# Two-layer vision network in one program: the routing of layer 0's mixture of experts is rewritten and its slot writes leave their critical sections

## The chip, the cores and the metric

The kernel runs on one core of a Trainium2 chip, as one program with one launch. The metric is the device time of one execution in microseconds (us); the median of three runs stands for a kernel. Beside the times there is one execution recorded by the hardware profiler, with every instruction of the five engines: PE (TensorE, matrix products), DVE (VectorE), ACT (ScalarE), POOL (GpSimd) and SP (SyncE, which here only starts DMA transfers). "ACTq", "POOLq" and the like are the instruction queues of an engine, from which DMA transfers are started too.

## The reference, cut to what matters

The network has two layers, each a token mixer and a mixture of experts, on 4 images of 256 channels and 32 x 32 positions (4096 tokens in all). Layer 0 mixes by attention and then sends each token to the best two of eight experts. Each layer normalises the tokens ahead of this, without gain or bias; then:

```python
logits = tokens.astype(jnp.float32) @ router_w.astype(jnp.float32).T
probs = jax.nn.softmax(logits, axis=-1)
rw, re = jax.lax.top_k(probs, TOP_K)
if TOP_K > 1:
    rw = rw / jnp.maximum(rw.sum(-1, keepdims=True), 1e-12)
...
for e in range(E):
    h = jax.nn.gelu(tokens @ w1[e] + b1[e], approximate=False)
    y = h @ w2[e] + b2[e]
    out = out + combine[:, e:e + 1] * y
```

The two weights are the probabilities of the best two, divided by their sum. Written with the logits l1 >= l2 of the two they are 1 / (1 + exp(l2 - l1)) and exp(l2 - l1) / (1 + exp(l2 - l1)): the softmax over all eight cancels. And since a token's mean is the same for all channels, the product of the centred token with the router is the product of the token itself with router weights whose mean over the channels has been taken out.

## The kernel before, in words

Notation: P = 128 partitions, C = 256 channels in CT = 2 halves, L = 1024 positions of an image in NT = 8 tiles of 128 tokens, B = 4 images, E = 8 experts. The activations of all images stay in SBUF, as x[b], 128 x (2 x 1024), channels on partitions.

The program has stages that follow each other: normalisation and attention of layer 0; the routing of layer 0; its experts (tiles of 256 slots); the scans of layer 1, which carry the routing of layer 1 beside them; the experts of layer 1; the output. Attention and scans are emitted in an order written out by hand. The routing and the experts of layer 0 are emitted plainly, and the framework's scheduler decides the order of the instructions within each engine; it also inserts the semaphores, and it gives the DMA transfers of POOL eight semaphores in turn. A buffer pool with a given number of buffers makes a new tile wait until the oldest one is free. After attention a conditional block (line 1021) holds a second, slower attention, which is not taken here; the routing comes behind it.

**Routing of one image** (loop at line 1543, per image): `norm` (line 1253) multiplies x[b] by a matrix of 1/C on PE, which gives each token's mean on all partitions (L1262); DVE subtracts it (L1265) into d; PE transposes d, so that tokens lie on partitions (L1274), and multiplies d by the router weights rw0 (L1276); DVE copies the logits out of PSUM (L1278), ACT copies the rows into `tok` (L1279), and squares them with a running sum for the variance (L1282). The inverse root comes from ACT's Sqrt (L1290), a reciprocal on DVE (L1292) and one Newton step (L1293 to L1296). Logits (L1301) and rows (L1304, ACT, 8 instructions) are multiplied by it. `route` (line 1131) makes the softmax (L1158 to L1163, its Exp on ACT at L1160), and takes the best expert twice (`best`, L1150 to L1154). The weights of both go into columns C + 1 and C + 2 of the row (L1176 to L1181). Then it counts, by two products on PE (L1193, L1194) and running sums on DVE (L1197 to L1213), which place of its expert each token gets; the slot numbers go as integers into `here` (L1217 to L1219). The logits of all images lie in one tile, lg1; `here` and the scratch tile `numbers` have one buffer too.

**Slot writes.** Each row is 259 numbers long: 256 channels, the best expert's number and two weights. POOL writes the rows of an image into the slots of their experts in DRAM (slots_x0): 8 tiles x 2 choices = 16 transfers of 128 rows each, with addresses from `here` (L1557). They stand in a critical section (L1554) on POOL, at whose end POOL waits until all 16 have landed:

```python
with tc.tile_critical(name=f"scatter{b}", no_gpsimd_drain=True):
    for n in range(NT):
        for k in range(2):
            nc.gpsimd.indirect_dma_start(
                out=slots_x0, out_offset=bass.IndirectOffsetOnAxis(ap=here[:, k, n : n + 1], axis=0),
                in_=tokens[b][:, n], in_offset=None).then_inc(scattered, 16)
    nc.gpsimd.wait_ge(scattered, 16 * 2 * NT * (b + 1))
```

**Experts of layer 0** (line 1656 on): `load` (L1583 to L1588) starts, on SP and in this order, the rows of a tile, then its two weight matrices; PE transposes the rows (L1594), multiplies by w1 (L1616), ACT takes the GELU (L1618), PE multiplies by w2 (L1624), DVE and ACT add bias and weight (L1627 to L1632), POOL starts the store (L1634). The first tile needs the rows of all images. Other small loads that the change touches are started on ACT, by the helper `load` at line 83 (L85): the weights of the attention at the start of the program, and at the start of the routing those of the scans (wd, wbc, bd, dskip, a_log) and the bias b1_0.

## Time and profile before

| | us |
|---|---|
| median of three runs | 4119.95 |
| the three runs | 4119.56, 4119.95, 4127.55 |
| the profiled execution, its time | 4116.54 |
| its span, from first to last instruction | 4114.8 |
| attention's last addition to x, ended | 1899.1 |
| first matmul of the routing (L1262) | 1904.73 |
| first and last slot write (L1557), started | 1937.46, 2039.19 |
| first load of an expert tile's rows (L1583), started | 2042.63 |
| first GELU of layer 0's experts (L1618) | 2049.41 |

Over the whole span PE is busy for 86%, DVE for 74%, ACT for 69% and POOL for 43%. A page of the profile gives these shares for the whole, and in 40 slices of 103 us each; the routing lies in slices 19 and 20. In a timeline each line is: start, duration, engine, line of the program, operation, output and inputs, count; and in brackets the idle time of the engine before it and what ended that. In the list of waits a line says who waited for whom, the total, the number of times and the longest. The release that is named is inferred: where a wait had several conditions, it is the one that came last in the record.

### The profile page before, as it was taken

How to read it: one execution, taken by the hardware profiler on the slowest of the kernel's cores; microseconds unless marked ns; L12 is line 12 of the kernel's file. 1: busy time of each engine (PE TensorE's matmuls, PEld its weight loads, DVE VectorE, ACT ScalarE, POOL GpSimd, SP SyncE). 2: the span in 40 equal slices, each digit the busy share in tenths (PEclk: the TensorE clock that was granted, in tenths of full speed). 3: DMA queues.
4: the chain of work that ended last, by engine and by line, in shares of the span. 5: the costliest groups of instructions: out<-in, count | busy, mean ns of one | idle time of the engine just before them, and what ended most of it. 6: DMA issues, size and time to landing. Idle time of an engine off the chain costs nothing. (4 is left out here: it accounts for less than half of the span.)

```text
span 4114.8 us, 50233 instructions
## 1 busy us (share of the span) xinstructions
PE 3526.9 (86%) x17502; PEld 1947.5 (47%) x17502; DVE 3032.4 (74%) x5416; ACT 2828.4 (69%) x3805; POOL 1785.3 (43%) x1435
## 2 busy tenths in 40 slices
PE   8378888888888888965388999999999999999996
PEld 5134444444344434433275444444444434688885
DVE  2689899989898989893466899899899899411112
ACT  2889999999999999973234676767667677422222
POOL 0145444554455445552433656445445446121111
PEclk9568787888778877887699999999999999999997
DMA  9300093000000000000384434333323334555565
GB/s 288 97 1 1 1 255 90 1 1 19 1 1 1 11 1 1 10 2 31 107 241 140 133 110 133 103 108 125 107 99 124 117 102 138 187 183 190 189 194 181
DMA packets 241817, 393.33 MB, mean 96 GB/s; under 512 B 31889, under 2 KB 182162, under 8 KB 241426
## 3 DMA queue, kind: packets, MB, share of 16 engines
q1 hardware_dynamic: 217872, 340.19, 27.3%
q0 software_dynamic: 19904, 48.42, 3.6%
q8 instruction: 141, 2.31, 0.2%
q10 hardware_dynamic: 3778, 1.41, 0.1%
q14 instruction: 122, 1.00, 0.1%
HBM read 280.34 MB, written 109.61 MB: 95 GB/s over the span
## 5 line engine op out<-in xcount | busy, mean ns | idle before, releaser
L491 POOL TENSOR_SCALAR dr<-s_n,last 128x1024 bf16<-128x1024 f32 x256 | 733.0, 2883 | 853.7 <-DVE state L519 392.3
L407 ACT ACTIVATE junk_a<-s_n,state 128x1024 int8<-128x1024 f32 x448 | 514.6, 1149 | 24.8 <-DVE state L525 7.5
L1768 POOL TENSOR_TENSOR da_c<-prod,come 128x1024 f32<-128x1024 f32 x128 | 247.5, 1934 | 436.1 <-DVE h L1774 376.4
L411 DVE TENSOR_SCALAR_CACHE_REDUCE junk_v<-s_n,state 128x1024 int8<-128x1024 f32 x320 | 408.6, 1277 | 8.8
L1944 ACT ACTIVATE hid<-hp,b 128x256 f32<-128x256 f32 x288 | 133.8, 474 | 356.2 <-PE hp L1942 353.3
L458 DVE SCALAR_TENSOR_TENSOR w<-s_n,win 128x1024 f32<-128x1024 f32 x256 | 349.2, 1364 | 5.3
L461 DVE MAX8 win<-w 128x8 f32<-128x1024 f32 x256 | 314.5, 1228 | 8.9
L559 ACT ACTIVATE ex<-sT 128x1024 f32<-128x1024 f32 x256 | 247.0, 1015 | 87.3 <-PE sT L551 87.2
L1735 POOL TENSOR_TENSOR uu<-dx,bb 128x1024 f32<-128x1024 f32 x127 | 302.3, 2380 | 1.9 <-DMA bb<-bc_d 1.7
L407 ACT ACTIVATE junk_a<-s_n,guess 128x1024 int8<-128x1024 f32 x256 | 294.2, 1149 | 7.4
L1774 DVE TENSOR_TENSOR_SCAN h<-da_c,uu 128x1024 f32<-128x1024 f32 x127 | 288.7, 2273 | 0.0
L1748 DVE TENSOR_TENSOR_SCAN h<-da,uu 128x1024 f32<-128x1024 f32 x127 | 288.4, 2271 | 0.0
L1757 DVE TENSOR_TENSOR_SCAN h<-da,uu 128x1024 f32<-128x1024 f32 x127 | 287.4, 2263 | 0.0
L569 PE MATMUL o_ps<-ex,vT 128*32 128x256 f32 x2048 | 241.5, 451 | 46.2 <-ACT ex L559 38.8
L1719 ACT ACTIVATE da_c<-delta,a_log 128x1024 f32<-128x1024 f32 x128 | 268.4, 2097 | 6.6 <-issue 6.5
L1778 PE MATMUL hp<-h,ident 128*128 128x512 f32 x512 | 250.4, 612 | 22.8 <-DVE h L1774 22.6
L1942 PE MATMUL hp<-xe,w 128*128 128x256 f32 x1152 | 258.8, 381 | 7.3 <-DVE xe L1930 7.1
L441 ACT COPY s_n<-sp 128x1024 f32<-128x1024 f32 x256 | 245.4, 1003 | 22.4 <-PE sp L433 11.5
L1953 DVE TENSOR_TENSOR ys<-yp,b2e 128x512 f32<-128x512 f32 x36 | 24.9, 692 | 319.6 <-PE yp L1950 319.6
L1950 PE MATMUL yp<-w2e,hid 128*128 128x256 f32 x1152 | 255.9, 379 | 0.0
L1743 PE MATMUL hp<-da_c,ident 128*128 128x512 f32 x512 | 248.8, 609 | 6.3 <-POOL da_c L1768 3.6
L1736 ACT COPY uu<-uu 128x1024 f32<-128x1024 f32 x127 | 252.5, 1988 | 1.6 <-POOL uu L1735 1.6
(570 smaller groups left out, 7471.6 us busy)
## 6 DMA issues: line engine op xcount, KB each, us to landing
cb<-bc_d SPq DMA_DIRECT2D x128, 512.0 KB
bb<-bc_d SPq DMA_DIRECT2D x127, 512.0 KB
w<-in_w SPq DMA_DIRECT2D x36, 1024.0 KB
w2e<-in_w SPq DMA_DIRECT2D x36, 1024.0 KB
slots_x<-zeros SPq DMA_DIRECT2D x1, 33411.0 KB
slots_x<-zeros SPq DMA_DIRECT2D x1, 33282.0 KB
w<-in_w SPq DMA_DIRECT2D x72, 256.0 KB
xs<-slots_x SPq DMA_DIRECT2D x36, 259.0 KB
```

The lines of the kernel that those rows point to most:

```text
L407: nc.scalar.activation(junk, self.row(r), AF.Sign, bias=thr, scale=-1.0, accum_out=u)
L411: nc.vector.tensor_scalar(junk, self.row(r), thr, None, ALU.is_lt, ALU.add, accum_out=u)
L458: nc.vector.scalar_tensor_tensor(w, self.row(r), self.win[:, r, 0:1], self.row(r), ALU.is_gt if r < LAST_DVE else ALU.is_ge, ALU.subtract, ...
L461: nc.vector.max(out=self.win[:, r, 1:], in_=w)
L491: ins = nc.gpsimd.tensor_scalar(dr, self.row(r), self.last[:, r : r + 1], None, ALU.is_lt)
L1719: nc.scalar.activation(grid(self.da_c), cols_flipped(self.prep.delta[:, self.c]), AF.Exp, scale=self.decay)
L1735: nc.gpsimd.tensor_tensor(self.uu[:, 0], self.prep.dx[:, self.c], self.bb, ALU.mult)
L1748: nc.vector.tensor_tensor_scan(rows.rearrange("p r w -> p (r w)"), self.da, self.uu[:, 0], 0.0, ALU.mult, ALU.add)
L1757: nc.vector.tensor_tensor_scan(hs[:, ::-1], self.da[:, ::-1], self.uu[:, 0][:, ::-1], 0.0, ALU.mult, ALU.add)
L1774: nc.vector.tensor_tensor_scan(hs, self.da_c, self.uu[:, 1], 0.0, ALU.mult, ALU.add)
L1942: nc.tensor.matmul(hp[:, f % 2], self.w1[:, c, ts(f, P)], self.xe[:, c], start=(c == 0), stop=(c == CT - 1))
L1950: nc.tensor.matmul(yp[:, a], self.hid[:, f, ts(a, P)], self.w2[:, f, :], start=(f == 0), stop=(f == NF - 1))
```

## The change

- The router weights are loaded at the very start of the program, their mean over the channels is taken out (two products on PE, one subtraction on DVE), and a ninth column of 1/C is added: one product of a token with it gives the logits and the mean.
- A new function `normed0` takes the place of `norm` in layer 0. It works on x[b] directly: products with the nine columns for all tiles of an image in one PSUM tile (`raw`, two buffers), transposes into three buffers `t`; DVE makes minus the mean from the ninth column, ACT copies the rows and squares them with the mean as a bias. The inverse root is made on DVE alone, by a first guess from the bits and three Newton steps. ACT then scales and shifts the rows (8 instructions).
- `route` in layer 0 takes the best two from the logits. One Exp, of l2 - l1, 8 numbers per token row, is left, and the weights are made from it after the counting products.
- Logits, `here`, scratch and small tiles have two or four buffers, where they had one.
- The critical sections go. The 64 slot writes are declared as free of dependences on each other ("rows of their own"); the loads of the experts wait for them by the framework's semaphores.
- Six small loads (wd, wbc, bd, dskip, a_log, b1_0) move from ACT's queue to SP's, ahead of the load of b2_0.

In the order that the build gives, PE makes the products of image 1 between those of image 0, and a slot write waits for the one eight before it, for ACT's scaling of its rows and for `here`. `norm` keeps layer 1's part, with its argument for the layer taken away; the two calls that follow from this are left out below.

```diff
     nc.gpsimd.iota(zeros[:, C : C + 1], [[0, 1]], base=2 * B * L, channel_multiplier=2,
                    allow_small_or_imprecise_dtypes=True)
 
+
+    rw0 = cons.tile([P, CT, E + 1], F32, tag="rw0", name="rw0")
+    nc.vector.memset(rw0[:, :, E:], 1.0 / C)
+    with tc.tile_pool(name="w_ps", bufs=1, space=PSUM) as pool_p, tc.tile_pool(name="w_sb", bufs=1) as pool_s:
+        raw0 = load(pool_s, "raw0", [P, CT, E], t["rw0"].rearrange("(c p) o -> p c o", p=P))
+        mean = pool_p.tile([P, E], F32, tag="mean", name="mean")
+        for c in range(CT):
+            nc.tensor.matmul(mean, mean_w, raw0[:, c], start=(c == 0), stop=(c == CT - 1))
+        nc.vector.tensor_tensor(rw0[:, :, :E], raw0, mean.unsqueeze(1).to_broadcast([P, CT, E]), ALU.subtract)
 
     kf = cons.tile([P, 1], F32, tag="kf", name="kf")
...
     rt = ctx.enter_context(tc.tile_pool(name="rt", bufs=1))
     rw1 = load(cons, "rw1", [P, CT, E], t["wr1"].rearrange("(c p) o -> p c o", p=P))
     brs = load(cons, "brs", [P, E], t["br1"][0].partition_broadcast(P))
-    rw0 = load(cons, "rw0", [P, CT, E], t["rw0"].rearrange("(c p) o -> p c o", p=P))
     def kept(name, shape, dt=F32):
         return rt.tile([P, *shape], dt, tag=name, name=name)
...
     every, early, late = Tiles("every", NTILE), Tiles("early", EARLY), Tiles("late", NTILE - EARLY)
     extra = rt.tile([1, 1], I32, tag="extra", name="extra")
 
-    def route(b, layer, tok, slot, space, psum, tag, keep_hots=None, keep_rank=None):
+    def route(b, layer, tok, slot, space, psum, tag, lg1=lg1, keep_hots=None, keep_rank=None):
 
 
         used = 0
...
             nc.vector.tensor_reduce(red, eq, AX.X, ALU.max)
             nc.vector.tensor_tensor(hot, eq, red.unsqueeze(2).to_broadcast(wide), ALU.is_equal)
 
-        if layer == 0:
-
-            nc.vector.tensor_reduce(m1, lg1, AX.X, ALU.max)
-            nc.vector.tensor_tensor(lg1, lg1, m1.unsqueeze(2).to_broadcast(wide), ALU.subtract)
-            nc.scalar.activation(lg1, lg1, AF.Exp)
-            nc.vector.tensor_reduce(m1, lg1, AX.X, ALU.add)
-            nc.vector.reciprocal(m1, m1)
-            nc.vector.tensor_tensor(lg1, lg1, m1.unsqueeze(2).to_broadcast(wide), ALU.mult)
-        else:
+        if layer == 1:
             nc.vector.tensor_tensor(lg1, lg1, brs.unsqueeze(1).to_broadcast(wide), ALU.add)
         best(m1, hot1)
         yield
...
         nc.vector.scalar_tensor_tensor(lg1, hot1, -1e30, lg1, ALU.mult, ALU.add)
         best(m2, hot2)
         hots = (hot1, hot2)
-        if layer == 0:
-            nc.vector.tensor_tensor(red, m1, m2, ALU.add)
-            nc.vector.tensor_scalar(red, red, 1e-12, None, ALU.max)
-            nc.vector.reciprocal(red, red)
-            nc.vector.tensor_tensor(m1, m1, red, ALU.mult)
-            nc.vector.tensor_tensor(tok[:, :, C + 2], m2, red, ALU.mult)
-            nc.vector.tensor_tensor(tok[:, :, C + 1], m1, tok[:, :, C + 2], ALU.subtract)
-        else:
-            nc.vector.tensor_tensor(m2, m2, m1, ALU.subtract)
-            nc.scalar.activation(m2, m2, AF.Exp)
-
+        nc.vector.tensor_tensor(m2, m2, m1, ALU.subtract)
+        nc.scalar.activation(m2, m2, AF.Exp)
         both, tote, keep, cum = room([NT, E]), room([E, NT]), room([E, NT]), room([E, NT])
         nc.vector.tensor_tensor(both, hot1, hot2, ALU.add)
         yield
...
         nc.vector.tensor_scalar(tote, sums[:, 1].rearrange("p n e -> p e n"), float(C), None, ALU.mult)
         nc.vector.tensor_copy(place, sums[:, 0].rearrange("p n e -> p e n"))
         yield
-        if layer == 1:
+        if layer == 0:
+            nc.vector.tensor_scalar(red, m2, 1.0, None, ALU.add)
+            nc.vector.reciprocal(m1, red)
+            nc.vector.tensor_tensor(tok[:, :, C + 2], m2, m1, ALU.mult)
+            nc.vector.tensor_tensor(tok[:, :, C + 1], m1, tok[:, :, C + 2], ALU.subtract)
+        else:
             nc.vector.tensor_scalar(m1, m2, 1.0, None, ALU.add)
             nc.vector.reciprocal(wts[:, 0, ts(b, NT)], m1)
             nc.vector.tensor_tensor(wts[:, 1, ts(b, NT)], m2, wts[:, 0, ts(b, NT)], ALU.mult)
...
             ends = late.fill(room, tiles, done)
             nc.vector.tensor_scalar(extra, ends[0:1, E - 1 : E], USUAL - EARLY + 0.5, None, ALU.is_gt)
 
-    def norm(b, layer, tok, pool, psum, tag, raw_tag, d):
-
-
-
-        rw = (rw0, rw1)[layer]
+    def normed0(b, tok, lg, pool, psum):
+
+        raw = psum.tile([P, HALF], F32, tag="raw", name="raw")[:, : NT * (E + 1)].rearrange(
+            "p (n e) -> p n e", e=E + 1)
+        ve, rr, r0, rs, nm = (pool.tile([P, NT], F32, tag=f"n0_{i}", name=f"n0_{i}")
+                              for i in ("ve", "rr", "r0", "rs", "nm"))
+        for r in range(NT // 2):
+            tp = psum.tile([P, 2, C], F32, tag="t", name="tp", bufs=3)
+            for i in range(2):
+                n = 2 * r + i
+                for c in range(CT):
+                    nc.tensor.matmul(raw[:, n], x[b][:, c, ts(n, P)], rw0[:, c, :], start=(c == 0), stop=(c == CT - 1))
+                for c in range(CT):
+                    nc.tensor.transpose(tp[:, i, ts(c, P)], x[b][:, c, ts(n, P)], ident)
+            nc.vector.tensor_scalar(nm[:, ts(r, 2)], raw[:, ts(r, 2), E], -C ** -0.5, None, ALU.mult)
+            nc.scalar.copy(tok[:, ts(r, 2), :C], tp)
+            for i in range(2):
+                n = 2 * r + i
+                nc.scalar.activation(tp[:, i], tp[:, i], AF.Square, bias=nm[:, n : n + 1], scale=C ** -0.5,
+                                     accum_out=ve[:, n : n + 1])
+        nc.vector.tensor_scalar(ve, ve, 1e-5, None, ALU.add)
+        nc.vector.tensor_scalar(r0.bitcast(I32), ve.bitcast(I32), -0.5, RSQRT_BITS, ALU.mult, ALU.add)
+        for src, dst in ((r0, rs), (rs, r0), (r0, rs)):
+            nc.vector.tensor_tensor(rr, src, src, ALU.mult)
+            nc.vector.scalar_tensor_tensor(rr, rr, -0.5, ve, ALU.mult, ALU.mult)
+            nc.vector.scalar_tensor_tensor(dst, rr, 1.5, src, ALU.add, ALU.mult)
+        nc.vector.tensor_tensor(lg, raw[:, :, :E], rs.unsqueeze(2).to_broadcast([P, NT, E]), ALU.mult)
+        nc.vector.scalar_tensor_tensor(nm, nm, C ** 0.5, rs, ALU.mult, ALU.mult)
+        for n in range(NT):
+            nc.scalar.activation(tok[:, n, :C], tok[:, n, :C], AF.Identity, bias=nm[:, n : n + 1],
+                                 scale=rs[:, n : n + 1])
+
+    def norm(b, tok, pool, psum, tag, raw_tag, d):
+
+
+
+        rw = rw1
         for h in range(NHALF):
             cols = ts(h, HALF)
             mean = psum.tile([P, HALF], F32, tag=tag, name="nm_mean")
...
         nc.vector.tensor_scalar(ve, var, 1e-5, None, ALU.add)
         yield from rsqrt(s1)
-        if layer == 0:
-            nc.vector.tensor_tensor(lg1, lg1, s1.unsqueeze(2).to_broadcast([P, NT, E]), ALU.mult)
-            yield
-            for n in range(NT):
-                nc.scalar.mul(tok[:, n, :C], tok[:, n, :C], s1[:, n : n + 1])
-            yield
-            return
-
         nc.vector.tensor_tensor(ve, s1, s1, ALU.mult)
         nc.vector.tensor_tensor(ve, ve, var, ALU.mult)
         nc.vector.tensor_scalar(ve, ve, 1e-5, None, ALU.add)
...
     sd = of_scans.enter_context(tc.tile_pool(name="s_d", bufs=2))
     sw = of_scans.enter_context(tc.tile_pool(name="s_c", bufs=1))
     bc_dram = ctx.enter_context(tc.tile_pool(name="s_dram", bufs=2, space=bass.MemoryType.DRAM))
-    wd = load_rows(sw, "wd", C)
-    wbc = load_rows(sw, "wbc", 2 * NS)
-    bd = load(sw, "bd", [P, CT])
-    dsk = load(sw, "dskip", [P, CT])
-
-    am = load(sw, "a_log", [P, CT, NS])
+    wd = load_rows(sw, "wd", C, nc.sync)
+    wbc = load_rows(sw, "wbc", 2 * NS, nc.sync)
+    bd = load(sw, "bd", [P, CT], eng=nc.sync)
+    dsk = load(sw, "dskip", [P, CT], eng=nc.sync)
+
+    am = load(sw, "a_log", [P, CT, NS], eng=nc.sync)
     nc.scalar.activation(am, am, AF.Exp)
     nc.vector.tensor_scalar(am, am, -1.0, None, ALU.mult)
     twice = sw.tile([P, P], F32, tag="twice", name="twice")
...
     with ExitStack() as st:
         wp = st.enter_context(tc.tile_pool(name="m0_w", bufs=1))
-        b1 = load(wp, "b1_0", [P, E, CT])
+        b1 = load(wp, "b1_0", [P, E, CT], eng=nc.sync)
         b2 = wp.tile([P, E, C], F32, tag="b2_0", name="b2_0")
         nc.sync.dma_start(b2, t["b2_0"].rearrange("e d -> (e d)").partition_broadcast(P).rearrange(
             "p (e d) -> p e d", e=E))
...
         with ExitStack() as sr:
             pr = sr.enter_context(tc.tile_pool(name="r0_w", bufs=1))
             pd = sr.enter_context(tc.tile_pool(name="r0_b", bufs=2))
-            ps_n = sr.enter_context(tc.tile_pool(name="r0_ps", bufs=3, space=PSUM))
-            tokens = [pr.tile([P, NT, W0], F32, tag=f"tok{b}", name=f"tok{b}") for b in range(B)]
-            scattered = nc.alloc_semaphore("scattered")
+            ps_n = sr.enter_context(tc.tile_pool(name="r0_ps", bufs=2, space=PSUM))
             for b in range(B):
                 hots0.append([wp.tile([P, NT, E], F32, tag=f"hot{b}{k}", name="hot") for k in range(2)])
                 rank0.append(wp.tile([P, E, NT], F32, tag=f"rank{b}", name="rank"))
-                d = pd.tile([P, CT, L], F32, tag="d", name="d")
-                here = pr.tile([P, 2, NT], I32, tag="here", name="here")
-                for _ in norm(b, 0, tokens[b], pd, ps_n, "t", "t", d):
+                rows = pr.tile([P, NT, W0], F32, tag=f"tok{b}", name="rows")
+                lg = pd.tile([P, NT, E], F32, tag="lg", name="lg")
+                here = pd.tile([P, 2, NT], I32, tag="here", name="here", bufs=B)
+                normed0(b, rows, lg, pd, ps_n)
+                numbers = pd.tile([P, 1408], F32, tag="numbers", name="numbers")
+                for _ in route(b, 0, rows, here, numbers, ps_n, "r", lg, hots0[b], rank0[b]):
                     pass
-                numbers = pr.tile([P, 1408], F32, tag="numbers", name="numbers")
-                for _ in route(b, 0, tokens[b], here, numbers, ps_n, "t", hots0[b], rank0[b]):
-                    pass
-
-                with tc.tile_critical(name=f"scatter{b}", no_gpsimd_drain=True):
-                    for n in range(NT):
-                        for k in range(2):
-                            nc.gpsimd.indirect_dma_start(
-                                out=slots_x0, out_offset=bass.IndirectOffsetOnAxis(ap=here[:, k, n : n + 1], axis=0),
-                                in_=tokens[b][:, n], in_offset=None).then_inc(scattered, 16)
-                    nc.gpsimd.wait_ge(scattered, 16 * 2 * NT * (b + 1))
-                    if b == B - 1:
-                        nc.clear_and_free_semaphores([scattered])
+                for n in range(NT):
+                    for k in range(2):
+                        ins = nc.gpsimd.indirect_dma_start(
+                            out=slots_x0, out_offset=bass.IndirectOffsetOnAxis(ap=here[:, k, n : n + 1], axis=0),
+                            in_=rows[:, n], in_offset=None).ins
+                        tc.declare_no_dep(ins, group="scatter0", reason="rows of their own")
+                        tc.add_to_no_dep_group("scatter0", ins)
 
         pb = st.enter_context(tc.tile_pool(name="m0_b", bufs=2))
         ps_n = st.enter_context(tc.tile_pool(name="m0_ps_n", bufs=3, space=PSUM))
```

More of the change, by code (lines that the diff above doesn't have):

```diff
@@ L86, in load, with load_rows @@
         return w
-    def load_rows(pool, name, cols):
-        return load(pool, name, [P, CT, cols], t[name].rearrange("(c p) o -> p c o", p=P))
+    def load_rows(pool, name, cols, eng=None):
+        return load(pool, name, [P, CT, cols], t[name].rearrange("(c p) o -> p c o", p=P), eng)
     def layer_norm_steps(dst, src, eps, room, psum, tag):
@@ L1811, in routed @@
             nonlocal sending
-            yield from norm(b, 1, tok, p1, ps_m, "hp", "hp", p1.tile([P, CT, L], F32, tag="xm", name="nm_d"))
+            yield from norm(b, tok, p1, ps_m, "hp", "hp", p1.tile([P, CT, L], F32, tag="xm", name="nm_d"))
             yield from route(b, 1, tok, slot, p1.tile([P, NUMBERS], F32, tag="numbers", name="numbers"), ps_m, "hp")
@@ L1976, in metaformer @@
             b = B - 1
-            routing = chain(norm(b, 1, tok, pa, psa, "t", "raw", pa.tile([P, CT, L], F32, tag="nm_d", name="nm_d")),
+            routing = chain(norm(b, tok, pa, psa, "t", "raw", pa.tile([P, CT, L], F32, tag="nm_d", name="nm_d")),
                             route(b, 1, tok, slot, pa.tile([P, NUMBERS], F32, tag="numbers", name="numbers"), psa, "t"), scatter(b))
```

## The prediction

> **What bounds the kernel now.** I read the page for the shares by slice, the waits and the timelines of each engine around the routing of layer 0, and the windows by stage. The page's chain of work that ended last is almost all from the last stage, so the routing has to be judged in its own window. Attention ends at 1899, the branch after it costs until 1904.7, the first tile of layer 0's experts is loaded at 2042.6. In most of those 138 us all engines are lightly used:
>
> ```profile
> core 0: us, PE busy (x) PEld busy (x) DVE busy (x) ACT busy (x) POOL busy (x), PEclk, DMA share, GB/s
> 1937.00:2042.00 105.00, 34.66 (x178) 26.48 (x176) 36.95 (x193) 36.27 (x96) 61.79 (x64) 0.61 0.23 81
> ```
>
> POOL is the busiest, with the 64 slot writes (L1557), and even it idles. The waits of 1900 to 2045 (waiter, what released it, total us, times, longest):
>
> ```profile
> ACT L1618 <- POOLq L1554: 33.0, 1, 33.0
> POOL slots_x L1557 <- PE nm_mean L1262: 31.1, 1, 31.1
> POOL slots_x L1557 <- issue: 18.3, 60, 0.3
> POOL slots_x L1557 <- DVE d L1265: 14.5, 2, 8.2
> POOL slots_x L1557 <- SPq L1638: 8.1, 1, 8.1
> ```
>
> The first line is the experts' start: it waits for POOL's last critical section. POOL's own timeline shows the rest: within an image one write per 1.265 us (0.96 busy, 0.30 between), between images a hole.
>
> ```profile
> 1937.46 1.26 POOL L1557 DMA_INDIRECT slots_x<-tok,here  x1 [31.09 <-PE nm_mean L1262]
> 1939.02 0.97 POOL L1557 DMA_INDIRECT slots_x<-tok,here  x1 [0.30 <-issue]
> ...
> 1963.98 0.96 POOL L1557 DMA_INDIRECT slots_x<-tok,here  x1 [6.25 <-DVE d L1265]
> ...
> 1992.16 0.96 POOL L1557 DMA_INDIRECT slots_x<-tok,here  x1 [8.25 <-DVE d L1265]
> ...
> 2020.21 0.96 POOL L1557 DMA_INDIRECT slots_x<-tok,here  x1 [8.13 <-SPq L1638]
> ...
> 2039.19 0.96 POOL L1557 DMA_INDIRECT slots_x<-tok,here  x1 [0.30 <-issue]
> ```
>
> So the period of an image (1937.46, 1963.98, 1992.16, 2020.21: 26.5 to 28.2 us) is not POOL's 16 x 1.265 = 20.2 us but the image's arithmetic, which is done one image after another. In that arithmetic one stall stands out, image 1's on ACT and DVE:
>
> ```profile
> 1944.59 1.28 ACT L1290 ACT_TABLE_LOAD   x1
> 1947.17 3.30 ACT L1304 ACTIVATE tok<-tok,nm_s 128x256 f32<-128x256 f32 x8 [1.08 <-DVE nm_sd L1295]
> 1950.48 1.28 ACT L1160 ACT_TABLE_LOAD   x1
> 1951.78 0.26 ACT L1160 ACTIVATE lg<-lg 128x64 f32<-128x64 f32 x1
> 1952.07 0.22 DVE L1161 TENSOR_REDUCE numbers<-lg 128x8 f32<-128x64 f32 x1 [4.16 <-ACT lg L1160]
> ```
>
> The softmax's exponential stands behind eight row scalings and a table load, and DVE waits 4.16 us for it.
>
> **What the Trainium skill says.** "ScalarE activation tables: per-element evaluation and per-set limits", What a function is on this engine: functions of two sets are one table load of 1283 ns apart. The trace agrees: 1.28 us, two per image. "Perfetto Trace Analysis", DMA Instruction — SWDGE (GPSIMD): a POOL DMA's recorded end is that of writing descriptors, not of the data. It agrees: the last record ends at 2040.15 and the experts' first instruction, which waits for the data, runs at 2042.36. "DMA: Bandwidth & Descriptors", Anatomy of one DMA — SWDGE (gpsimd) path: 2.0 us plus bytes/436e3; for 128 rows x 259 x 4 B = 132.6 KB I estimate 2.3 us, near the 2.2 seen here. "SBUF — State Buffer", SBUF: two separate sides: some DVE operations lock POOL out of writing descriptors. No lengthening shows here: the writes keep 0.96 us while DVE works on the next image.
>
> **The change, part by part.** All four images run through the same engines in order; what counts is when image 0's first write starts, and whether POOL then ever waits.
>
> *Image 0, up to its first write* (before: 1904.73 to 1937.46). Removed: the mean matmuls (PE 1904.73 to 1910.2) and the subtraction d (two pairs of DVE operations, 1.29 us each), the softmax: two operations ahead of the exponential (0.5), the stall of 4.16, three after it (0.75), some 5.4 us in all; and the entry of the critical section: the slots were ready at 1935.40 but the write began at 1937.46, when PE's mean matmul of image 1 had ended: 2.1 us. Added: in the built order PE does the logits of image 1 (8 tiles x about 0.55 us = 4.5) before image 0's last transposes, and DVE takes three Newton steps. So, engine by engine: PE needs for image 0 some 7 us of work (from 1910.08 to 1919.0 less 2 us of waits), plus 4.5 for image 1, plus about 0.5 of waits for DVE between: transposes done near 1916.7. ACT then copies two tiles (2 x 0.59) and squares three halves (3 x 0.56): 1919.6, where before the last square ended at 1919.4. So the mean gains nothing: image 1 eats it. Eleven small DVE operations at 0.2 us (L1293 to L1296 are 0.20 apart): 1921.8, against 1922.0 before: Newton costs what root, table load and reciprocal did. Scaled logits and mean 0.4: 1922.2. The two best-of steps, 3.1 us as before (1927.65 to 1930.78): 1925.3. Sums on PE and back, 1.3 as before (1930.78 to 1932.11): 1926.6. To the first slots: 2.6 before (1932.11 to 1934.70), plus one operation for image 2 and four for the weights, which come here now, at some 0.15: 3.3, so 1929.9. The exponential (of 8 numbers per row) starts after the eight row operations; these begin when Newton ends, at 1921.9, plus 3.3 + 0.26 = 1925.5, ahead of DVE's need at about 1928.3, so nothing waits. First write: **1930**, 7.5 us earlier. Bounds: 1927 (PE not slowed by image 1) to 1934 (clock low in the alternating logits, which cost 1.7 rather than 1.0 us per pair of tiles at 1917.29).
>
> *The holes.* POOL needs image 1's slots at 1930 + 20.2 = 1950. DVE's work per image is about 48 operations at 0.22 = 10.5 us plus PE's 1.3; ACT's is 4 x 1.7 (copy and squares) + 3.3 + 0.3 = 10.4. DVE ends image 0 at 1931 and image 1 near 1944, 6 us in hand; images 2 and 3 near 1957 and 1970, needed at 1970 and 1991. So the holes go: 6.25 + 8.25 + 8.13 - 3 x 0.30 = **21.7 us**. From then on POOL's 64 x 1.265 = 81 us bound the stage.
>
> *Waits that are added.* In the built order each write waits for the one eight before (eight semaphores in turn), and for ACT's row. Eight writes are 10.1 us; the data need 2.2. Upper bound: layer 1's last writes, which wait for the one directly before:
>
> ```profile
> 3604.66 0.97 POOL L1685 DMA_INDIRECT slots_x<-tok,slot  x1 [0.30 <-DVE late_which L1090]
> 3607.96 0.97 POOL L1685 DMA_INDIRECT slots_x<-tok,slot  x1 [2.33 <-DMA slots_x<-tok,slot]
> ```
>
> The first followed its predecessor by 1.27 with its waits met; I take that, so 64 x 0.005 = 0.3, and up to 1.5. Behind a waiting write stand only the next writes, and SP, which waits for all eight semaphores before it loads the first tile's rows.
>
> *End of the stage.* 1930 + 63 x 1.27 + 0.96 = 2011. Before, load followed the last record by 2.48 us (2040.15 to 2042.63), through the critical section; now SP waits for the data itself, 2.2. I book no gain.
>
> *Start of the kernel.* The router load and two matmuls stand first; by the built order the load of wqk waits for them (its buffer is theirs): about 3 us for wqk, wv, wproj. The image's load, which PE waits for until 8.41, then shares the DMA engines with less, and bp moves behind the four mean matmuls. Cover: PE's wait to 8.41. Bounds -2 and +3; I take 0. The six loads moved from ACT to SP (4.4 us of ACT issue, 1905.15 to 1909.57) free ACT, which waited for PE until 1910.4 anyway: 0. On SP only the bias load b2 stands behind them; nobody needs it before the experts: 0. a_log still lands before ACT is through image 0's third pair (1912.7).
>
> *Experts of layer 0.* PE's order differs in the first few tiles: -2 to +2, taken 0.
>
> Sum: -7.5 - 21.7 + 0.3 = **-28.9 us**. The profiled execution: span 4114.8 to 4085.9, its time 4116.54 to 4087.6. The median of the three runs is 3.4 above that time: 4119.95 - 28.9 = **4091**.
>
> **Rivals.** (1) *Holes stay, though smaller*: ACT and DVE interleave two images and wait for each other in order (DVE's mean for image 2 stands before image 0's weights and waits for ACT). For it: DVE stood still without work shown for 6.0 and 6.1 us before L1278 of images 2 and 3 (1975.34, 2002.75). Against: 6 us in hand at image 1, 13 and more later. If each image costs 25 us, three holes of 4.8 return: -14.5, 4105. (2) *Later stages absorb it*: with 29 us less of idle TensorE, which has only 0.61 of the clock here, the later grant falls; 29 us in the 2072 after the stage are 1.4% of clock. Against: the grant was 0.95 right after the stage. Then 4119. (3) *Slower: the writes still wait for each other*, since the declaration doesn't hold or data land late. At layer 1's 3.3 us per write 64 take 211 us instead of 102.7, less 7.5 at the front: +101, 4221. It decides from a spacing of (102.7 + 7.5)/64 = 1.72 us, which with eight in flight needs landings over 13.8 us. Against: the built order waits at distance eight, and 2.2 us are seen.
>
> **How the numbers follow.** Main case 0.75 (its own range 4083 to 4099: first write 1927 to 1934, start -2 to +3, experts ±2, and ±3 of run-to-run), rival 1 0.17 (4098 to 4111), rival 2 0.04, rival 3 0.04. The time is the main case's; the range, 4080 to 4108, takes in most of rival 1. A change within 0.2% (8 us; the three runs spread over 8) is no change: rival 2. Faster 0.92, same 0.04, slower 0.04.
>
> **What would show it.** Right: 64 writes 1.27 us apart in one row, the first near 1930, the last near 2010; no table load before the experts; rows loaded near 2013; later stages 29 us earlier and as long as before. Wrong: idle before the 17th, 33rd or 49th write (rival 1, its releaser names the engine), idle before most (rival 3), a later first matmul than 8.4, or a lower grant after 2013 (rival 2).

## The result, and the profile after

The median went from 4119.23 us (ten runs) to 4088.53 us (ten runs): ratio 0.9928, with a 95% interval of 0.9910 to 0.9945. The profiled execution of the changed kernel took 4087.82 us, its span is 4085.5 us; before they were 4116.54 and 4114.8. The mean granted TensorE clock (the share of full speed that the throttle allows, called the grant below) is 0.878, before 0.879. The prediction was 4091, and 4087.6 for the profiled execution. The sum was right to 0.4 us, but not all of its parts were, and that the first row came out at -0.3 is chance: the executions below begin the routing at anything from 1895.4 to 1923.2. The ratio's interval stands for 23 to 37 us.

| stretch | before, us | after, us | difference | predicted |
|---|---|---|---|---|
| up to the first product of the routing | 1904.73 | 1904.44 | -0.3 | 0 |
| from there to the first slot write | 32.73 | 30.39 | -2.3 | -7.5 |
| first to last slot write | 101.73 | 79.98 | -21.75 | -21.4 |
| last slot write to first GELU | 10.22 | 9.97 | -0.25 | 0 |
| first GELU to the end of POOL's last store record | 2056.6 | 2055.4 | -1.2 | 0 |
| after that, to the span's end | 8.8 | 5.3 | -3.5 | 0 |
| sum | | | -29.3 | -28.9 |

POOL's timeline of the kernel after, from the first write to the last; the lines are the 1st write, the 16th and 17th, the 33rd, for which the write eight before it is named, and the last (start, duration, engine, line, operation; in brackets the idle time before it and what ended that):

```profile
1934.83 1.26 POOL L1573 DMA_INDIRECT slots_x<-rows,here  x1 [29.34 <-ACT tp L1267]
...
1954.10 0.96 POOL L1573 DMA_INDIRECT slots_x<-rows,here  x1 [0.30 <-issue]
1955.36 0.96 POOL L1573 DMA_INDIRECT slots_x<-rows,here  x1 [0.30 <-issue]
...
1975.60 0.96 POOL L1573 DMA_INDIRECT slots_x<-rows,here  x1 [0.30 <-DMA slots_x<-rows,here]
...
2014.81 0.96 POOL L1573 DMA_INDIRECT slots_x<-rows,here  x1 [0.30 <-issue]
```

1955.36 is the first write of image 1: where 6.25 us of idle time stood before, there are 0.30. All 64 writes are 1.27 us apart. The list of POOL's waits, same kernel (total, times, longest), says the same: where a wait on another write is named, it is never longer than the 0.3 that stand between any two writes.

```profile
POOL slots_x L1573 <- ACT tp L1267: 29.3, 1, 29.3
...
POOL slots_x L1573 <- issue: 13.1, 43, 0.3
...
POOL slots_x L1573 <- DMA slots_x<-rows,here: 3.4, 11, 0.3
```

So the queue that bounds the stage now never waits; its start is what is left to gain. The start came late on PE. PE's timeline of the kernel after:

```profile
1904.44 0.99 PE L1260 MATMUL raw<-rw,x 128*128 128x9 f32 x4 [5.69 <-PEq L1030]
1905.29 0.67 PE L1262 MATMUL tp<-ident,x 128*128 128x128 f32 x2
1905.75 0.86 PE L1260 MATMUL raw<-rw,x 128*128 128x9 f32 x4
1906.46 2.38 PE L1262 MATMUL tp<-ident,x 128*128 128x128 f32 x10
1908.63 11.96 PE L1260 MATMUL raw<-rw,x 128*128 128x9 f32 x56
1920.43 2.80 PE L1262 MATMUL tp<-ident,x 128*128 128x128 f32 x12
```

The 64 records of the nine-column product are those of images 0 and 1; they take 13.7 us and stand ahead of image 0's last transposes. And they are slower than those of before. The windows by stage (stretch, its length, busy time of PE, weight load, DVE, ACT, POOL with counts, then the granted clock, the DMA share, GB/s), first of the kernel before, then of the kernel after:

```profile
1904.70:1910.20 5.50, 5.47 (x10) 2.43 (x11) 2.91 (x15) 0.00 (x0) 1.10 (x8) 0.66 0.73 245
1910.20:1919.40 9.20, 7.25 (x49) 6.60 (x47) 2.10 (x9) 5.94 (x21) 0.00 (x0) 0.78 0.04 9
```

```profile
1904.40:1908.60 4.20, 4.16 (x20) 4.19 (x21) 1.69 (x14) 1.17 (x2) 1.10 (x8) 0.50 0.39 86
1908.60:1920.50 11.90, 11.90 (x59) 11.90 (x58) 1.00 (x8) 3.70 (x15) 0.00 (x0) 0.50 0.26 88
```

Before, dense products (the means, 512 columns wide) opened the stage and the grant was 0.66 and then 0.78. After, they are gone, PE is busy without a gap by the record, and the grant stays at 0.50. (The kernel one_raw below has no dense products either, and its grant does rise.)

The end of the stage is as foretold, only later: SP starts the rows of the first tile at 2017.69, 2.9 us after the last write began, and ACT loads a table, where there were eight loads in the routing before, for the first time since attention (timeline of ACT, after):

```profile
2017.94 1.28 ACT L1633 ACT_TABLE_LOAD   x1 [46.48 <-DVE b1e L1616]
2024.78 0.47 ACT L1633 ACTIVATE hid<-hp,b1e 128x256 f32<-128x256 f32 x1 [5.55 <-PE hp L1631]
```

The last 3.5 us were not in the forecast. They lie at the end of the program, in POOL's final DRAIN, an instruction that starts 0.04 us after the record of POOL's last store ends. By source line, durations min/median/max in ns; kernel before, then after:

```profile
L2092 POOLq DRAIN  x3: 51/98/7954, 4106.0 to 4114.5; - x3
```

```profile
L2107 POOLq DRAIN  x3: 46/118/4524, 4080.1 to 4085.2; - x3
```

### The profile page after: what moved, and what is told of

Its sections match the earlier page's. It is cut to its first block, busy times and chain, and to the rows that moved or that the text cites. A ratio compares the mean times of both kernels' runs of the same rounds, so it can differ in the third digit from the quotient of the medians.

```text
span 4085.5 us, 50150 instructions
## 1 busy us (share of the span) xinstructions
PE 3517.2 (86%) x17474; PEld 1957.8 (48%) x17474; DVE 3022.1 (74%) x5402; ACT 2819.9 (69%) x3793; POOL 1787.2 (44%) x1435
```

## The experiments

The first question was what the change's two halves, the arithmetic and the freed writes, are worth alone; the second, how the first write comes earlier; the third, what the long waits are that showed up on the way. All stage times are in us after the stage's own first product on PE, because that product starts up to 28 us apart in these executions, though the code ahead of it is nearly the same. They come from one profiled execution of each row. A time is a median, and a ratio is to the kernel before in runs on the same chip; the medians of the kernel before in these sets are 4112.68 to 4133.51, so that rows are compared by their ratios, not by their times. Where there is no ratio, there is one execution only.

| kernel | first write | last write | first GELU | POOL idle before writes 17, 33, 49 | time | ratio |
|---|---|---|---|---|---|---|
| before | 32.7 | 134.5 | 144.7 | 6.25, 8.25, 8.13 | | 1 |
| after | 30.4 | 110.4 | 120.3 | none | 4088.53 | 0.9928 (0.9910 to 0.9945) |
| critical | 32.7 | 124.3 | 134.6 | 4.01, 4.09, 4.04 | 4108.93 | 0.9950 (0.9932 to 0.9968) |
| freed | 29.8 | 149.1 | 158.8 | 7.14, 15.46, 17.64 | 4148.03 | 1.0033 (1.0016 to 1.0049) |
| again_freed | 30.4 | 151.9 | 161.6 | 7.55, 17.46, 17.55 | 4142.52 | 1.0045 (1.0031 to 1.0059) |
| one_raw | 25.9 | 122.4 | 133.1 | none, 16.59, none | 4106.00 | 0.9951 (0.9929 to 0.9974) |
| slots_first | 20.3 | 123.9 | 133.9 | none, 17.56, 6.62 | 4103.42 | 0.9943 (0.9921 to 0.9964) |
| again_slots_first | 20.3 | 100.4 | 109.9 | none | 4080.79 | 0.9915 (0.9883 to 0.9947) |
| again_after | 30.4 | 110.6 | 120.2 | none | 4092.55 | 0.9944 (0.9919 to 0.9969) |
| single | 26.2 | 114.4 | 126.7 | 3.13, 5.32, none | 4093.77 | 0.9919 (0.9893 to 0.9944) |
| before_again | 32.1 | 133.1 | 143.3 | 5.71, 8.29, 7.82 | 4116.83 | |
| chained | 30.4 | 232.5 | 243.2 | each write waits | 4206.82 | |
| writes_last | 53.6 | 133.5 | 145.7 | none | 4130.37 | |
| freed_last | 105.3 | 185.5 | 201.1 | none | 4182.03 | |

**The arithmetic alone (critical).** The kernel after, with its writes put back into four critical sections:

```diff
+                with tc.tile_critical(name=f"scatter{b}", no_gpsimd_drain=True):
                     for n in range(NT):
                         for k in range(2):
-                            ins = nc.gpsimd.indirect_dma_start(...).ins
-                            tc.declare_no_dep(ins, group="scatter0", reason="rows of their own")
-                            tc.add_to_no_dep_group("scatter0", ins)
+                            nc.gpsimd.indirect_dma_start(...).then_inc(scattered, 16)
+                    nc.gpsimd.wait_ge(scattered, 16 * 2 * NT * (b + 1))
```

> One part of the change undone: the 64 slot writes stand in their four critical sections again; the new arithmetic and the double buffers stay. Theory A (the shorter arithmetic of an image is what closes the holes, the freed writes add the rest): an image's slots are ready every 15.3 us, so POOL never waits for arithmetic, only for its own section's end. Each section lasts 16 x 1.265 = 20.2 us plus a landing of about 2.2 us and a fresh entry, so 22.5 to 23.5 us per image: three holes of 2.5 to 3.5 us instead of 0, first write at 1935 to 1937, last at about 2022 to 2026, 8 to 12 us over the changed kernel: median about 4097 to 4101. Rival B (it was the sections that held the images apart): the holes of 6 to 8 us come back, last write at 2034 or later, 4110 or more.

The stage is 10.1 us shorter than before, against 24.3 for the whole change. Image by image, POOL pays for the end of a section (timeline of POOL, critical):

```profile
1964.50 0.96 POOL L1575 DMA_INDIRECT slots_x<-rows,here  x1 [4.01 <-ACT rows L1264]
...
1988.58 0.96 POOL L1575 DMA_INDIRECT slots_x<-rows,here  x1 [4.09 <-DVE numbers L1158]
...
2012.62 0.96 POOL L1575 DMA_INDIRECT slots_x<-rows,here  x1 [4.04 <-issue]
```

Three holes of 4.0 us, alike although the releasers named differ: this fits the section's own wait for its 16 landings and the entry of the next, not an engine that is late. They are 3 x 3.7 = 11.2 us over the usual 0.30, and the first write is 2.3 later than after: 13.5 of the 14.2 us between this kernel and after. ACT and DVE have "remote" waits here too (explained with the next kernel), 20.5 us in all; the holes, alike as they are, hide them. The runs as a whole give the arithmetic more: a ratio of 0.9950 is 13 to 28 us (its interval), where the stage of this one execution shows 10.1. Its interval overlaps those of the kernel after and of again_after. What freeing the writes adds to the new arithmetic is thus seen in the stage, in one execution of critical, and is not settled in the time of the whole program. Its final DRAIN is long again:

```profile
L2110 POOLq DRAIN  x3: 51/98/7957, 4102.1 to 4110.6; - x3
```

In all kernels with critical sections (before, before_again, critical) it takes 7.954 to 7.957 us, in the eleven without 4.52 to 4.53. So 3.4 us of the change come from the sections, with the semaphore that they count on, being gone, 2000 us after the routing.

**The freed writes alone (freed, again_freed).** The kernel before, with `here` in four buffers and the same declaration in place of the section:

```diff
-                here = pr.tile([P, 2, NT], I32, tag="here", name="here")
+                here = pr.tile([P, 2, NT], I32, tag="here", name="here", bufs=B)
-                with tc.tile_critical(name=f"scatter{b}", no_gpsimd_drain=True):
...
+                        tc.declare_no_dep(ins, group="scatter0", reason="rows of their own")
+                        tc.add_to_no_dep_group("scatter0", ins)
```

> One part of the change alone: the kernel before with its slot writes freed of the critical sections and with four buffers for the slot numbers; the old norm, softmax and single buffers stay. Theory A: an image still takes 26 to 28 us of arithmetic and POOL 20.2, so the holes stay at about 6 to 8 us; only the entry (2.1 us at image 0) and the exit of the sections go: first write at 1935.4, last at 2034 to 2037, 2 to 5 us under the kernel before: median 4114 to 4118. Rival B: the holes go with the sections, last write at about 2016, median about 4096.

> The kernel before with its writes freed, once more. Its first profile took 158.8 us from first product to first GELU against 144.7 of the kernel before, with seven stalls of DVE of 4 to 10 us. Theory S (stalls belong to the execution): fewer stalls this time, holes of 3 to 7 us before each image, 134 to 145 us, median 0 to 10 us under the kernel before. Theory O (freed writes beside the old arithmetic always bring the stalls): 155 us or more again, median 8 us or more above the kernel before.

It is slower than before, twice: 1.0033 and 1.0045, the intervals above 1. POOL starts 2 to 3 us sooner and then waits more. DVE's waits of again_freed say for what:

```profile
DVE lg L1278 <- remote: 42.6, 5, 13.2
```

"remote" stands where the view finds no releaser among the engines; the line is DVE's copy of the logits out of PSUM. The input that it reads, the product on PE, had long been done: in freed the longest wait, of 10.47, ends at 2000.99, and the last product of that image had ended at 1993.2. Such a wait is called a late release from here on. freed has the same line with 39.9 us in six. Before has 6.0 and 6.1 us at that line for images 2 and 3, and before_again 6.00 and 5.50 at the same places.

So in the stage the two halves don't add: -10.1 for the arithmetic, +14 to +17 for the writes, -24.3 for both.

**Where the freed kernel's time goes (freed_last).** freed, with all slots copied once by POOL ahead of all writes, so that no write is under way while the images are worked on:

```diff
+            nc.gpsimd.tensor_copy(late_here, all_here)
+            for b in range(B):
+                here = late_here[:, b]
```

> The kernel before with freed writes and one POOL copy of all slot numbers ahead of them, so that no write stands beside the old arithmetic. It measures that arithmetic by itself. Theory A (the holes of the kernel before are its arithmetic of 26.5 us per image): the fourth image's slots 107 to 111 us after the first product, last write 80 us later. If most of the 26.5 us were delays by the writes beside it (22 us or less per image): 97 us or less. Theory W: no stall of DVE or ACT without a release in the record.

No wait of the "remote" kind is left in the routing. POOL's timeline of freed_last, where the copy marks the end of all four images' arithmetic:

```profile
2021.85 0.23 POOL L1555 COPY late_here<-all_here 128x64 int32<-128x64 int32 x1 [103.31 <-DVE all_here L1219]
2022.76 1.37 POOL L1560 DMA_INDIRECT slots_x<-tok,late_here  x1 [0.68 <-POOL late_here L1555]
```

The first write is 105.3 after the first product, 75 later than freed's: three images more, about 25 us each. That is the old arithmetic undisturbed, and it is more than POOL's 20.2 per image. With freed writes it would leave three holes of 4.8; freed has 7 to 18 us each. The rest is the late releases, which come with the writes.

**Image 1's products out of the way (one_raw).** One buffer for `raw`, so that image 1's products cannot stand ahead of image 0's transposes; the bank goes to `tp`:

```diff
-        raw = psum.tile([P, HALF], F32, tag="raw", name="raw")[...]
+        raw = psum.tile([P, HALF], F32, tag="raw", name="raw", bufs=1)[...]
-            tp = psum.tile([P, 2, C], F32, tag="t", name="tp", bufs=3)
+            tp = psum.tile([P, 2, C], F32, tag="t", name="tp", bufs=4)
```

> The changed kernel with one buffer for the logits' PSUM tile instead of two, and four instead of three for the transposes. By its built order PE then makes no product of image 1 before image 0's transposes, but makes all of image 1's before image 0's counting products. Theory P (the first write is late because 32 products of image 1 at 0.214 us stand ahead of image 0's transposes): the inverse root of image 0 starts 8 us earlier, near 1916.4; of this 4 us come back in front of the counting products; first write at 1930 to 1932 instead of 1934.8, still one write per 1.265 us, last at 2010 to 2012: about 4 us under the changed kernel. Rival Q (ACT's copies and squares or DVE set the first write): first write stays within 1 us of 1934.8.

The first write comes 4.5 us sooner than after's. More than the order is at work in this: with four buffers PE makes all 16 transposes of image 0 in the first 5.2 us, and then the grant rises, without any dense product. Windows of one_raw, up to the end of these transposes and behind it, where the other products of image 0 stand:

```profile
1899.50:1904.70 5.20, 5.20 (x26) 5.20 (x26) 1.71 (x15) 1.76 (x3) 1.04 (x8) 0.50 0.39 92
1904.70:1908.20 3.50, 3.00 (x26) 2.81 (x25) 0.32 (x2) 3.27 (x13) 0.00 (x0) 0.96 0.64 267
```

Eight records of the nine-column product take 1.06 us there, where they take 1.71 in the kernel after. Over the stage the gain is lost: 16.59 us of POOL ahead of write 33. DVE's timeline of one_raw in that stretch:

```profile
1950.37 0.17 DVE L1273 SCALAR_TENSOR_TENSOR n_rr<-n_rr,n_ve 128x8 f32<-128x8 f32 x1 [1.22 <-DVE n_rr L1272]
1951.77 0.17 DVE L1274 SCALAR_TENSOR_TENSOR n_rs<-n_rr,n_r 128x8 f32<-128x8 f32 x1 [1.23 <-DVE n_rr L1273]
...
1970.79 0.16 DVE L1263 TENSOR_SCALAR n_nm<-raw 128x2 f32<-128x2 f32 x1 [5.47 <-remote]
```

The Newton steps wait only for each other. In the kernel after they follow at 0.20 us; here at 1.40 over most of 1947 to 1961, with 0.17 of work in each. The releases come late even from DVE to itself.

**Slots first (slots_first, again_slots_first, and again_after beside the latter).** The slots need only the logits, and the best two of a row don't change when the row is scaled by its positive inverse root. So the products of an image come first, then `route` on the unscaled logits, and only then transposes, squares and root; l2 - l1 is multiplied by the root ahead of Exp:

```diff
-    nc.vector.memset(rw0[:, :, E:], 1.0 / C)
+    nc.vector.memset(rw0[:, :, E:], -C ** -1.5)
...
+        for n in range(NT):
+            for c in range(CT):
+                nc.tensor.matmul(raw[:, n], x[b][:, c, ts(n, P)], rw0[:, c, :], start=(c == 0), stop=(c == CT - 1))
+        nc.vector.tensor_copy(lg, raw)
+        for _ in routed:
+            pass
         ...
-        nc.vector.tensor_tensor(lg, raw[:, :, :E], rs.unsqueeze(2).to_broadcast([P, NT, E]), ALU.mult)
...
+        weights[0](rs, lg)
...
+                nc.vector.tensor_tensor(m2, m2, rs, ALU.mult)
+                nc.scalar.activation(m2, m2, AF.Exp)
```

The rest is buffers: `raw` and the counting sums share one PSUM bank, the transposes of four tiles share one PSUM tile of two banks, squares go to a scratch tile, and rows are scaled straight out of PSUM without ACT's copy.

> A rearranged version of the changed kernel: the best two are taken from the logits before the inverse root is known (a positive factor moves no maximum; only the difference is scaled, for the weights), all products of an image stand ahead of its transposes, the counting products share the logits' PSUM tile so that image 1's products can't come ahead of them, and ACT scales the rows straight from PSUM, without the copy. Theory P: slots of image 0 near 1919, root near 1921, weights near 1923, first write at 1922 to 1925, 10 to 12 us earlier than in the changed kernel; an image's arithmetic takes some 12 us, so POOL still writes without a hole, last write at 2002 to 2005; median about 4077, 0.27% under the changed kernel. Rival Q: ACT's squares and scalings set the pace, first write at 1930 or later, or holes come back because ACT must scale before PE may transpose the next image.

> The rearranged version (best two from unscaled logits, no copy, first write at 20.3 us after the first product) once more, unaltered. Theory S: the holes of 17.6 and 6.6 us before the 33rd and 49th write don't come back in the same places and sizes; without them the time from the first product to the first GELU would be about 110 us instead of 133.9. Theory O: the same two holes, within 2 us.

> The changed kernel once more, unaltered, for a second profile. Its first profile has no stall of DVE or ACT during the writes; the profiles of four other kernels have some, of 4 to 32 us, that end with no release in the record. Theory S (the stalls belong to the execution, not to the order of instructions): this second profile may show holes too, and the time from the first routing product to the first GELU, 120.3 us in the first profile, differs by more than 3 us. Theory O (the order decides): no hole again, 120 us within 1.

The first write is at 20.3 both times, 10.1 sooner than after. The first execution lost it again to one wait of 32 us, on DVE's copy out of PSUM. POOL had writes in hand until 1956.2, and then had none (timelines of slots_first, DVE and POOL):

```profile
1961.01 0.23 DVE L1265 COPY lg<-raw 128x72 f32<-128x72 f32 x1 [32.05 <-remote]
```

```profile
1915.71 1.26 POOL L1584 DMA_INDIRECT slots_x<-rows,here  x1 [19.15 <-ACT rows L1288]
...
1973.77 0.96 POOL L1584 DMA_INDIRECT slots_x<-rows,here  x1 [17.56 <-ACT rows L1288]
...
2000.32 0.96 POOL L1584 DMA_INDIRECT slots_x<-rows,here  x1 [6.62 <-ACT rows L1288]
```

In the second execution of the same kernel nothing of the sort happens, and the stage takes 109.9 against 144.7 before (timeline of POOL, again_slots_first):

```profile
1919.38 1.26 POOL L1584 DMA_INDIRECT slots_x<-rows,here  x1 [19.16 <-ACT rows L1288]
...
1999.48 0.96 POOL L1584 DMA_INDIRECT slots_x<-rows,here  x1 [0.30 <-DMA slots_x<-rows,here]
```

In the runs that stand side by side, its median is 4080.79 against 4092.55 of the kernel after, 11.8 us less, near the 10.3 of the stage. Its two ratios to before, 0.9943 and 0.9915, have intervals that overlap those of the kernel after; that it beats that kernel is likely, not settled.

**Is it the writes? (writes_last).** slots_first, with POOL's copy of all slots ahead of all writes, as in freed_last.

> The rearranged version with one POOL copy of all slot numbers ahead of the first write, so that no write starts before the slots of all four images are there. Theory W (DVE and ACT stall because POOL's writes are under way): without writes beside them no engine stalls, an image takes 12 to 14 us, the slots of the fourth are there 55 to 65 us after the first product, the last write 80 us later, first GELU at 145 to 155 us after the first product. Rival (the stalls come from the arithmetic's own waits): stalls of several us with no release appear here as well.

```profile
1972.89 0.23 POOL L1585 COPY late_here<-all_here 128x64 int32<-128x64 int32 x1 [51.59 <-DVE all_here L1222]
```

All four images' arithmetic is done 53 us after the first product, about 11.1 us per image ((53.6 - 20.3) / 3), and no wait is late. The arithmetic is thus much shorter than POOL's 20.2. That the writes bring the late releases rests more on freed_last than on this one execution, since again_slots_first had none with its writes under way.

**The writes in a chain (chained).** The kernel after, without the declaration:

```diff
-                        tc.declare_no_dep(ins, group="scatter0", reason="rows of their own")
-                        tc.add_to_no_dep_group("scatter0", ins)
```

> The changed kernel without the declaration that its slot writes are free of each other: each write waits for the one before to land. Third rival of the prediction: 3.3 us per write as at the end of layer 1, 64 writes in some 210 us, about 4088 + 130 = 4220. With a landing of only 2.4 us as in the changed kernel's record, 2.4 + 0.3 = 2.7 us per write and about 4180. With one write under way at a time, theory W also expects fewer stalls of DVE and ACT than in the other kernels.

```profile
1931.35 0.97 POOL L1573 DMA_INDIRECT slots_x<-rows,here  x1 [2.44 <-DMA slots_x<-rows,here]
...
2129.80 0.96 POOL L1573 DMA_INDIRECT slots_x<-rows,here  x1 [2.00 <-DMA slots_x<-rows,here]
```

3.21 us per write on average, the stage 122.8 us longer than after: the prediction's third rival, measured (4206.82; it was priced at 4221). Without the two lines of the declaration the change would be a loss. And there is no late release in this routing: with one write in flight at a time, in one execution, the writes didn't bring any.

**One buffer for rows' scratch (single).** The pool `r0_b` with one buffer instead of two, `here` still with four.

> The changed kernel with one buffer instead of two for logits, scratch and the small tiles of the norm (slot numbers keep four), so that an image can't start its means before the one ahead has scaled its rows. Theory A (what closes the holes is that an image's arithmetic has become shorter than POOL's 20.2 us, not that two images overlap): by the built order only 8 instead of 32 products of image 1 stand ahead of image 0's last transposes, first write 24 to 26 us after the first product instead of 30.4, an image takes some 16 us, no hole; first product to first GELU 114 to 117 us instead of 120.3. Rival (the overlap by double buffers is needed): holes of 2 us or more before the 17th, 33rd and 49th write, 120 us or more.

Its ratio, 0.9919, can't be told from after's. Holes of 3.13 and 5.32 were not expected. In the profile the first write comes 4.2 sooner and the last 4.0 later; one of ACT's waits is late by 6.67 us:

```profile
1961.16 0.59 ACT L1264 COPY rows<-tp 128x512 f32<-128x512 f32 x1 [6.67 <-remote]
```

With such a wait in it the run doesn't tell what the second buffer is worth.

**The kernel before once more (before_again).** Unchanged.

> The kernel before, unaltered, for a second profile. Theory S: the stalls of 6.0 and 6.1 us of DVE in images 2 and 3 are not in the same places; without them the holes before the 33rd and 49th write shrink from 8.2 to 2 to 6 us and the time from first product to first GELU from 144.7 to 133 to 143 us. Theory O: the same stalls, 144 to 146 us.

Stage, holes and DVE's two late releases come back within 1.4 us, at the same instructions. So these belong to the kernel, while slots_first's of 32 us was there in one execution and not in the next. No single account (a disturbance of one execution, or a property of the built order) fits both.

## Why the prediction was right, and where it was not

*The holes.* Right: they are gone, and first to last write is 21.75 us shorter, where -21.7 for the holes and +0.3 for added waits had been booked. The ground given was that each engine's work per image is under POOL's 20.2 us. It holds: the scaled logits of images 0, 1 and 2 come at 1926.63, 1941.90 and 1957.08, 15.2 us apart, so DVE is 5 us further ahead with each image. The prediction had 13 us per image. The ground is not enough by itself, though: one_raw, single and one execution of slots_first have short arithmetic too, and late releases of an unknown cause brought holes of 3 to 17 us back. That the kernel after had none, in two executions, the prediction could not know; to that extent it was lucky. What it hadn't seen is that neither half does this alone: before's arithmetic takes 25.0 us per image even undisturbed, and with sections around the writes every image costs POOL 4.0 us at their ends.

*The waits on the write eight before.* Right: at most 0.3, the usual distance. The data landed 2.4/2.6/4.1 us (min/median/max) after issue; eight writes take 10.1.

*The first write.* Wrong in size: 1930 foretold, 1934.83 measured, beyond the stated bound of 1934. The step that failed is PE's time up to image 0's last transposes: some 7 us for image 0, plus 4.5 for image 1, done near 1916.7. They were done at 1921.4 (the first four of the twelve that begin at 1920.43). Both were priced by rows of before, the products at about 0.55 us per tile, among them

```profile
1913.88 0.51 PE L1276 MATMUL raw<-rw,d 128*128 128x8 f32 x4
```

from a stretch with a grant of 1.00: the window that gave 0.78 above has 1.00 up to 1914.70 and 0.56 behind that. In the kernel after PE runs at 0.50 throughout, and four such records take 0.86. Image 1's 32 records take 6.8 us instead of 4.5; image 0's own work takes 10.2 instead of 7, since its transposes ran at 0.50 as well; the 0.5 of waits did not come. That is 5.0 us, the whole shortfall. From the last square on (near 1924.4) the predicted 10.4 us to the first write were exact. The upper bound named the mechanism, a low clock, and was 0.8 us too low. Both prices stood in before's own rows: two tiles took 1.71 us at 1917.29, where its grant was 0.50.

The Trainium skill, "TensorE: Matmul & The Clock Gate", What's actually happening, says that the throttled clock is the default and that activity releases it, after about 3.4 us of a busy PE. The first half agrees with 0.50. The second does not: PE was busy for 11.90 of 11.90 us with nine-column products, and the grant stayed at 0.50. The measurement decides. What raises the grant is open. Dense products came ahead of the rise in before, but they are not needed: in one_raw it rose after a row of 14 transposes (3.23 us), and in slots_first, which spends 6.97 us on nine-column products at 0.50, it is 0.94 behind a row of 16 transposes (3.37 us). In the kernel after, the longest row up to 1920 is 10 transposes (2.38 us); the row of 12 at 1920.43 (2.80 us) was followed by no rise, while in again_after the same row was followed by 1.00. So it is likely the order of PE's work, as much as the loss of the dense products, that kept the clock low; no run changes one of these alone.

*Start and experts.* The start was 0 within 0.3. PE's first product on an image came 1.6 us sooner, at 6.82 instead of 8.41 (6.88 in again_after), but nothing of this can be seen at the routing, whose start scatters by far more. The experts and all that follows up to the last store gained 1.2, within the ±2 set for the experts; two executions of one kernel differ there by 3 (before and before_again, after and again_after), so it is no gain that can be told from zero.

*The end of the program.* Not in the sum at all: -3.4 from POOL's final DRAIN. With the -1.2 it makes up for most of the 5 us that were missing at the front. The total is right partly for that reason, that is, by luck.

*Rivals.* The first (holes stay) doesn't hold for after, though what spoke for it, DVE's standing still before L1278, was real: late releases left freed, one_raw and slots_first holes of 7 to 18 us. The second (a lower grant later) is out: 0.878 against 0.879. The third is what chained does.

## What to carry to other kernels

A stage in which one queue takes work from a chain of engines runs at the slower of the two periods: here the queue's 20.2 us against 25.0 of the old arithmetic and 15.2 of the new, and in the stage freeing the queue paid only once the chain was the faster one. Put what starts that queue ahead of what it doesn't need: the slots before the norm brought the first write 10 us forward, though in one of two executions a late release took that away again. And price small products by the clock at which they will run: a change that alters what PE does ahead of them, or in which order, can alter the grant, and rows taken at 1.00 are then too fast.

## What the runs showed of the hardware that was not expected

- Instructions of DVE and ACT that wait for PE, or DVE for itself, were released up to 32.05 us late. In the routing it was seen only while slot writes of POOL were under way side by side (none in writes_last and freed_last, nor in chained with one write at a time), in before at the same places in two executions, in slots_first in one of two, in neither execution of after. Some waits of up to 3.0 us of this kind stand in later stages. What holds the release back is not known; no run here tells a path.
- The final DRAIN of POOL takes 7.95 us in a program with the four critical sections and 4.52 without (critical and after).
- A PE that was busy without a gap for 11.9 us with 128x9 products kept a grant of 0.50; in one_raw, behind 5.2 us of 128x9 products and transposes, of which the last 3.23 us were transposes, it was 0.96, with no dense product ahead.
- A slot write of 128 rows costs POOL 1.265 us in a row, and 3.21 us when each waits for the one before.
